# The first 2 MB store of a one-core residual matmul, issued as four transfers of 16, 16, 32 and 64 partitions

## The chip, the core and the metric

The kernel runs on one core of one Trainium2 chip. The metric is device time in microseconds (us). The kernel before takes 323.31 us, the median of three runs that lie between 323.17 and 324.18 us.

The core has a matmul engine (TensorE, in the profile PE), a vector engine (VectorE, DVE), a scalar engine (ACT), GpSimd (POOL) and a sync engine (SP). Here ACT does no arithmetic: it only issues loads. SP only issues the two small loads at the start and all stores. The transfers themselves run on 16 DMA engines that all transfers share. The on-chip memory that tiles live in has 128 partitions; PSUM is the accumulator memory that TensorE writes.

## The reference

`x` is 128 batches of 128 channels by 1024 time steps in float32, 64 MB in all. Each batch has a subject number between 0 and 7, and each subject has a 128x128 weight matrix.

```python
def _L0_cond_ref(x, subjects, weights):
    w = weights[subjects]
    out = jnp.einsum('bct,bcd->bdt', x, w)
    return out
x = x + _L0_cond_ref(x, itok_B_0_7, L0_cond_weights)
```

So each batch is multiplied by the matrix of its subject and added to itself. Every byte of `x` is read once and every byte of the result written once.

## The kernel before

**Tiling.** The work is done in 32 turns (`NT`). A turn is four batches, in two halves of two (`H = 2`, `G = 2`). One batch is a 128 x 1024 float32 tile of 512 KB, so a turn is 2 MB: 16 KB on each of the 128 partitions. `x_all` is one long tile that holds 12 turns (`SLOTS = 12`), and turn `i` lives in slot `i % 12`. The result is written over the input in the same slot, and the slot is stored from there.

**What the engines do in a turn.** VectorE copies the four weight matrices that this turn needs into `w` (line 159). TensorE multiplies each half with eight matmuls of 512 columns (line 168). VectorE adds the product from PSUM to the slot (line 180), once for each half, and so makes the slot's result.

**The loads.** ACT issues one transfer for each batch, 128 of 512 KB (lines 206 to 210, through `load`). They all go to ACT's DMA queue, which the profile calls q10. The first 48 need no wait, since 12 slots are free. From turn 12 on, ACT waits before the four loads of a turn until the slot's earlier store has landed. How far the slot's semaphore must have counted is what `emptied(i)` gives: every transfer adds 16, so one round of a slot is four loads and one store, 80. In slot 0 two of the first turn's loads count on another semaphore (`s_head`), which is why the formula has an exception there.

**The stores.** SP issues them (lines 219 to 223) to its own DMA queue, q1 in the profile. It waits until VectorE has added the turn and, up to the last turns, four turns more (`BEHIND = 4`): the store of turn 0 goes out when turn 4 has been added. Turns 0 to 19 are stored one by one, 2 MB each; the last 12 turns go in pairs of 4 MB. One store takes all 128 partitions; on the memory side each partition's 16 KB are four rows of 4 KB, one in each of the four batches.

**The order around the change.** All of it is written out by hand. SP's instructions are the two small loads, then wait and store, turn by turn. ACT's are the loads in order of turn with the waits on the slots. GpSimd waits for each turn's loads and tells TensorE (lines 212 to 217). The last store waits for nothing but its data and ends the program (line 243 on).

Of the kernel before, what the change touches and what calls it, by code (L numbers as in the profile page):

```python
# [30 lines left out]
G = 2  # L31
H = 2
# [3 lines left out]
SLOTS = 12  # L36
# [9 lines left out]
DMA = 16  # L46

IDLE = 3

ROWS = 4  # L50

# [4 lines left out]
def transfer(nc, engine, out, in_):  # L56

    later, nc._always_lower_symbolic_ap = nc._always_lower_symbolic_ap, False  # L60
    ins, outs = engine.lower_ap_dma(in_), engine.lower_ap_dma(out)
    nc._always_lower_symbolic_ap = later
    return engine.add_instruction(
        mybir.InstDMACopy(
            name=nc.get_next_instruction_name(),
            engine=engine.engine,
            ins=ins,
            outs=outs,
            mode="Copy",
            cce_op=ALU.bypass,  # L70
            queue=QUEUES[engine.engine],
        )
    )
# [3 lines left out]
def kernel(  # L77
# [7 lines left out]
    nc = tc.nc  # L85
    B, C, T = x.shape
    S, _, D = weights.shape
    NT = B // (G * H)

    def sbuf(name, *shape, dtype=F32):  # L90
        return ctx.enter_context(nc.sbuf_tensor(name, list(shape), dtype)).ap()
# [5 lines left out]
    x_all = sbuf("x_all", C, SLOTS * H * G * T)  # L97
# [23 lines left out]
    s_slot = [tc.alloc_semaphore(f"s_slot{k}") for k in range(SLOTS)]  # L121
    s_head = tc.alloc_semaphore("s_head")

    def emptied(i):
        turns = i // SLOTS
        return DMA * (H * G + 1) * turns - (DMA * G if i >= SLOTS and i % SLOTS == 0 else 0)

    def load(engine, i, q):
        transfer(
            nc,  # L130
            engine,
            xs[i % SLOTS][:, q, :],
            x[i * H * G + q].rearrange("(a r) t -> a (r t)", r=ROWS),
        ).then_inc(s_head if i * H * G + q < G else s_slot[i % SLOTS], DMA)

    def store(i, n):
        at = i % SLOTS * H * G * T
        return transfer(
            nc,
            nc.sync,  # L140
            out[i * H * G : (i + n) * H * G].rearrange("g d t -> d g t"),
            x_all[:, at : at + n * H * G * T].rearrange(
                "d (o t) -> d o t", o=1 if i >= NT - WHOLE else n
            ),
        )

    def subjects_of(i):
        _, subject = nc.values_load_multi_w_load_instructions(
            index[0:1, i] if isinstance(i, slice) else index[0:1, bass.ds(i * (H * G), H * G)],
            engines=[mybir.EngineType.DVE],  # L150
            min_val=0,
            max_val=S - 1,
            skip_runtime_bounds_check_because="the index is clamped on the chip above",
        )
        return subject

    def place(h, subject):
        for q in range(h * G, (h + 1) * G):
            copy = nc.vector.tensor_copy(ws[q], w_all[:, bass.ds(subject[q], 1), :])  # L159
        copy.then_inc(s_go, 1)  # L160

    def multiply(slot, h):
        nc.tensor.wait_ge(s_go, 1).then_inc(s_go, -1)
        nc.tensor.wait_ge(s_ready, 1).then_inc(s_ready, -1)  # L164
        for q in range(h * G, (h + 1) * G):
            for t in range(0, T, N):
                at = slot * (H * G * T) + (q * T + t)
                mm = nc.tensor.matmul(  # L168
                    ps[h][:, q % G, t : t + N],
                    ws[q][:, 0, :],  # L170
                    x_all[:, bass.ds(at, N)],
                    start=True,
                    stop=True,
                )
        mm.then_inc(s_product, 1)

    def add(slot, h):
        mine = x_all[:, bass.ds(slot * (H * G * T) + h * G * T, G * T)]
        nc.vector.wait_ge(s_product, 1).then_inc(s_product, -1)  # L179
        nc.vector.tensor_tensor(  # L180
            mine, ps[h].rearrange("d g t -> d (g t)"), mine, ALU.add
        ).then_inc(s_added, 1)

    with tc.tile_critical():  # L184

        nc.sync.dma_start(given, subjects.rearrange("(o b) -> o b", o=1)).then_inc(s_given, DMA)
        nc.sync.dma_start(w_all, weights.rearrange("s c d -> c s d")).then_inc(s_wall, DMA)

        nc.vector.memset(zeros, 0.0).then_inc(s_zeros, 1)  # L189
        nc.tensor.wait_ge(s_zeros, 1)  # L190
        for _ in range(IDLE):
            nc.tensor.matmul(  # L192
                ps[P_SLOTS - 1][:, G - 1, :N], zeros[:, :D], zeros, start=True, stop=True
            )

        nc.vector.memset(index[:, B:], 0).then_inc(s_index, 1)  # L199
        nc.vector.wait_ge(s_given, DMA)  # L200
        nc.vector.tensor_scalar(near, given, -S, S - 1, ALU.max, ALU.min).then_inc(s_index, 1)  # L201
        nc.vector.wait_ge(s_index, 2)
        nc.vector.tensor_scalar(wrap, near, 0, S, ALU.is_lt, ALU.mult).then_inc(s_index, 1)  # L203
        nc.vector.wait_ge(s_index, 3)
        nc.vector.tensor_tensor(index[:, :B], near, wrap, ALU.add).then_inc(s_index, 1)  # L205
        for i in range(NT):
            if i >= SLOTS:
                nc.scalar.wait_ge(s_slot[i % SLOTS], emptied(i))
            for q in range(H * G):
                load(nc.scalar, i, q)  # L210

        for i in range(NT):
            if i == 0:
                nc.gpsimd.wait_ge(s_head, DMA * G).then_inc(s_ready, 1)
                nc.gpsimd.wait_ge(s_slot[0], DMA * G).then_inc(s_ready, 1)
            else:
                nc.gpsimd.wait_ge(s_slot[i % SLOTS], emptied(i) + DMA * H * G).then_inc(s_ready, H)

        for i in [*range(NT - SLOTS), *range(NT - SLOTS, NT, PAIR)]:
            n = 1 if i < NT - SLOTS else PAIR  # L220
            nc.sync.wait_ge(s_added, (i + n + (BEHIND if i < NT - LAST else 0)) * H)
            if i + n < NT:
                store(i, n).then_inc(s_slot[i % SLOTS], DMA)


        nc.vector.wait_ge(s_index, 4)
        nc.vector.wait_ge(s_wall, DMA)
        subject = subjects_of(slice(0, H * G))
        for h in range(H):
            place(h, subject)  # L230
        with nc.vector.Fori(0, NT) as turn:  # L231
            subject = subjects_of(turn + 1)
            for h in range(H):
                add(turn % SLOTS, h)
                place(h, subject)
        with nc.tensor.Fori(0, NT) as turn:
            for h in range(H):
                multiply(turn % SLOTS, h)

    with tc.tile_critical() as waits:  # L240
        for i in range(NT - SLOTS, NT - PAIR, PAIR):
            nc.scalar.wait_ge(s_slot[i % SLOTS], emptied(i + SLOTS))
# [35 lines left out]
```

## Time and profile before

| what | value |
|---|---|
| median of three runs | 323.31 us |
| lowest and highest run | 323.17 and 324.18 us |
| span of the profiled execution, first to last instruction | 322.2 us |
| TensorE busy | 246.3 us (76% of the span) |
| VectorE busy | 165.7 us (51%) |
| bytes moved by DMA | 134.76 MB, 418 GB/s over the span |
| stores, 2 MB: from issue to landing, median | 17.0 us |
| loads, 512 KB: from issue to landing, median | 30.7 us |

For the profiled execution the profile gives the span alone; it is 1.1 us under the median of the runs, which also hold what lies around the first and the last instruction. A time in a row of the profile is counted from the span's start. "DMA share" is the mean busy share of the 16 DMA engines in a stretch (values a little over 1 come from transfers that are booked to the stretch in which they begin), and "GB/s" is what they moved together. SPq and ACTq are the instructions with which SP and ACT issue transfers.

### The profile page before, as it was taken

The numbers are of one execution on the slowest core, as the hardware profiler recorded it, in microseconds if no ns is written. First come the engines' busy times: TensorE is split into PE (matmuls) and PEld (weight loads), VectorE is DVE, ScalarE is ACT, GpSimd is POOL, SyncE is SP. The second block draws the span as 40 slices with busy tenths as digits, with TensorE's granted clock in tenths as the row PEclk, the third lists the DMA queues.
The fourth block names the chain that finished last, engine by engine and source line by source line (L and its number), as shares of the span: only waits on it lengthen the run. The fifth ranks groups of instructions, "written<-read, shape, count | busy, mean of one in ns | idle before, by whom it ended". The sixth has DMA issues, their size and how long they took to land. (4 is left out here: it accounts for less than half of the span.)

```text
span 322.2 us, 2368 instructions
## 1 busy us (share of the span) xinstructions
PE 246.3 (76%) x518; PEld 101.8 (32%) x518; DVE 165.7 (51%) x202; POOL 0.2 (0%) x4
## 2 busy tenths in 40 slices
PE   6999999999996974975987489885699994972000
PEld 2344444444442421331333134332244431430000
DVE  2276776777677345354355344762657666254000
POOL 0000000000000000000000000000000000000000
PEclk9799999999999797797899899997999998698555
DMA  7999999999999999999999999999999999999996
GB/s 271 425 429 429 425 423 401 429 425 423 425 423 427 430 431 429 423 425 423 427 421 429 429 433 427 423 425 423 427 423 429 429 431 427 427 435 433 419 427 264
DMA packets 11315, 134.76 MB, mean 418 GB/s; under 512 B 2481, under 2 KB 3506, under 8 KB 3506
## 3 DMA queue, kind: packets, MB, share of 16 engines
q10 hardware_dynamic: 6144, 67.12, 49.6%
q1 hardware_dynamic: 5170, 67.64, 49.5%
q14 instruction: 1, 0.01, 0.0%
HBM read 67.63 MB, written 67.11 MB: 418 GB/s over the span
## 5 line engine op out<-in xcount | busy, mean ns | idle before, releaser
L168 PE MATMUL ps<-x_all,w 128*128 x512 | 241.3, 629 | 44.1 <-PEq L164 38.4
L180 DVE TENSOR_TENSOR x_all<-ps,x_all 128x2048 f32 x64 | 146.7, 2292 | 122.7 <-DVEq L179 122.7
L168 PEld LDWEIGHTS ps<-x_all,w 128*128 128x128 f32 x512 | 100.0, 201 | 185.7 <-issue 185.2
L159 DVE COPY w<-w_all 128x128 f32 x132 | 23.2, 219 | 4.7 <-DMA w_all<-in_L_cond_weights_dram 4.7
L192 PE MATMUL ps<-zeros 128*128 128x512 f32 x6 | 4.9, 988 | 1.7 <-DVE zeros L189 1.7
L192 PEld LDWEIGHTS ps<-zeros 128*128 128x128 f32 x6 | 1.8, 328 | 3.7 <-issue 2.1
L189 DVE MEMSET zeros<- 128x512 f32 x1 | 0.5, 485 | 1.0 <-SPq L184 1.0
L201 DVE TENSOR_SCALAR near<-given 1x128 int32<-1x128 int32 x1 | 0.2, 214 | 0.6 <-DMA given<-in_itok_B_dram 0.6
L205 DVE CUSTOM_DVE_ANT_0 index<-near,wrap 1x256 uint16<-1x256 uint16 x1 | 0.3, 280 | 0.0
L203 DVE TENSOR_SCALAR wrap<-near 1x128 int32<-1x128 int32 x1 | 0.2, 215 | 0.0
L265 POOL MEMSET const-bfloat16-1.0<- 128x1 bf16 x1 | 0.1, 102 | 0.0
L265 POOL MEMSET const-uint8-127<- 128x1 uint8 x1 | 0.1, 102 | 0.0
L265 POOL MEMSET const-float32-0.0<- 128x1 f32 x1 | 0.1, 99 | 0.2 <-issue 0.2
L265 POOL MEMSET const-float32-1.0<- 128x1 f32 x1 | 0.1, 99 | 0.0
L265 DVE BASE_LOAD x1 | 0.0, 21 | 0.1
L199 DVE MEMSET index<- 1x4 int32 x1 | 0.1, 62 | 0.0
## 6 DMA issues: line engine op xcount, KB each, us to landing
x_all<-in_x_dram ACTq DMA_DIRECT2D x128, 512.0 KB, 30.7
out_dram<-x_all SPq DMA_DIRECT2D x20, 2048.0 KB, 17.0
out_dram<-x_all SPq DMA_DIRECT2D x6, 4096.0 KB, 30.5
w_all<-in_L_cond_weights_dram SPq DMA_DIRECT2D x1, 512.0 KB, 5.5
given<-in_itok_B_dram SPq DMA_DIRECT2D x1, 0.5 KB
```

Source lines behind the costliest of these rows:

```text
L159: copy = nc.vector.tensor_copy(ws[q], w_all[:, bass.ds(subject[q], 1), :])
L168: mm = nc.tensor.matmul(ps[h][:, q % G, t : t + N], ws[q][:, 0, :], x_all[:, bass.ds(at, N)], start=True, stop=True,)
L180: nc.vector.tensor_tensor(mine, ps[h].rearrange("d g t -> d (g t)"), mine, ALU.add).then_inc(s_added, 1)
L189: nc.vector.memset(zeros, 0.0).then_inc(s_zeros, 1)
L192: nc.tensor.matmul(ps[P_SLOTS - 1][:, G - 1, :N], zeros[:, :D], zeros, start=True, stop=True)
L199: nc.vector.memset(index[:, B:], 0).then_inc(s_index, 1)
L201: nc.vector.tensor_scalar(near, given, -S, S - 1, ALU.max, ALU.min).then_inc(s_index, 1)
L203: nc.vector.tensor_scalar(wrap, near, 0, S, ALU.is_lt, ALU.mult).then_inc(s_index, 1)
L205: nc.vector.tensor_tensor(index[:, :B], near, wrap, ALU.add).then_inc(s_index, 1)
L265: nc = _bacc.Bacc("TRN2", target_bir_lowering=False, num_devices=1)
```

## The change

The store of turn 0, and only that, is issued as four transfers in place of one. They take partitions 0 to 15, 16 to 31, 32 to 63 and 64 to 127 of slot 0, each with all four batches: 256 KB, 256 KB, 512 KB and 1 MB. All four add to the slot's semaphore, so that turn 12's load waits for 96 instead of 48. No other instruction differs, on any engine.

```diff
 IDLE = 3
+
+PARTS = (16, 16, 32, 64)
...
     def emptied(i):
         turns = i // SLOTS
-        return DMA * (H * G + 1) * turns - (DMA * G if i >= SLOTS and i % SLOTS == 0 else 0)
+        first = DMA * (len(PARTS) - 1 - G) if i >= SLOTS and i % SLOTS == 0 else 0
+        return DMA * (H * G + 1) * turns + first
...
+    def store_rows(i, d, n):
+        at = i % SLOTS * H * G * T
+        return transfer(
+            nc,
+            nc.sync,
+            out[i * H * G : (i + 1) * H * G, d : d + n].rearrange("g d t -> d g t"),
+            x_all[d : d + n, at : at + H * G * T].rearrange("d (o t) -> d o t", o=1),
+        )
...
             nc.sync.wait_ge(s_added, (i + n + (BEHIND if i < NT - LAST else 0)) * H)
-            if i + n < NT:
+            if i == 0:
+                for k, rows in enumerate(PARTS):
+                    store_rows(i, sum(PARTS[:k]), rows).then_inc(s_slot[0], DMA)
+            elif i + n < NT:
                 store(i, n).then_inc(s_slot[i % SLOTS], DMA)
```

## The prediction

> **What bounds the kernel now.** I read the page's slices and queues first, because 134.76 MB in 322.2 us is suspiciously close to a plain copying rate.
>
> ```profile
> span 322.2 us, 2368 instructions
> ...
> DMA  7999999999999999999999999999999999999996
> GB/s 271 425 429 429 425 423 401 429 425 423 425 423 427 430 431 429 423 425 423 427 421 429 429 433 427 423 425 423 427 423 429 429 431 427 427 435 433 419 427 264
> DMA packets 11315, 134.76 MB, mean 418 GB/s; under 512 B 2481, under 2 KB 3506, under 8 KB 3506
> ## 3 DMA queue, kind: packets, MB, share of 16 engines
> q10 hardware_dynamic: 6144, 67.12, 49.6%
> q1 hardware_dynamic: 5170, 67.64, 49.5%
> ```
>
> The 16 DMA engines are busy in every slice but the first and the last, at 420 to 435 GB/s, whichever queue feeds them. One slice in the middle stands out: the seventh, 401 GB/s, which is 48.3 to 56.4 us. So I asked for the same numbers by stages.
>
> ```profile
> core 0: us, PE busy (x) PEld busy (x) DVE busy (x) POOL busy (x), PEclk, DMA share, GB/s
> 2.00:6.00 4.00, 4.00 (x5) 1.50 (x5) 0.71 (x3) 0.00 (x0) 1.00 1.00 322
> 6.00:46.00 40.00, 37.83 (x83) 15.58 (x82) 23.69 (x31) 0.00 (x0) 0.96 1.01 426
> 46.00:51.00 5.00, 5.00 (x12) 2.15 (x12) 3.78 (x4) 0.00 (x0) 1.00 1.00 423
> 51.00:56.00 5.00, 5.00 (x13) 2.01 (x11) 3.90 (x6) 0.00 (x0) 1.00 1.00 387
> 56.00:66.00 10.00, 10.00 (x25) 4.28 (x24) 7.24 (x7) 0.00 (x0) 1.00 0.99 423
> 66.00:116.00 50.00, 45.01 (x99) 18.54 (x97) 33.11 (x40) 0.00 (x0) 0.97 1.01 428
> 116.00:284.00 168.00, 131.97 (x272) 54.45 (x272) 85.66 (x103) 0.00 (x0) 0.92 1.01 426
> 284.00:320.00 36.00, 7.13 (x16) 2.96 (x16) 7.12 (x9) 0.00 (x0) 0.67 0.99 420
> 320.00:322.20 2.20, 0.00 (x0) 0.00 (x0) 0.00 (x0) 0.00 (x0) 0.50 0.00 0
> ```
>
> From 6 to 320 us the rate is that of saturated engines: about 426 GB/s with loads alone (6 to 46), with both kinds (66 to 284) and nearly so with stores alone (284 to 320). TensorE and VectorE have idle time in every long stage. The consequence for the sum: any microsecond in which all 16 engines move nothing comes back at the end as a microsecond, and a transfer that is merely earlier or later, while the other queue has work, costs nothing. The one place of waste in the middle is 51 to 56 us: 387 instead of 426 GB/s over 5 us, that is 5 x (1 - 387/426) = 0.46 us. What happens there is the first store:
>
> ```profile
> engine op xcount: duration ns min/median/max, first and last start us, forms
> L63 SPq DMA_DIRECT2D out_dram<-x_all x1: 652/652/652, 48.4 to 48.4; - x1
> ...
> DMA to landing us min/median/max: 14.1/14.1/14.1
> ```
>
> ```profile
> 45.45 17.53 ACTq L63 DMA_DIRECT2D x_all<-in_x_dram  x2
> ```
>
> ```profile
> 52.00:53.00 1.00, 1.00 (x4) 0.25 (x3) 0.34 (x3) 0.00 (x0) 1.00 0.49 180
> 245.00:250.00 5.00, 5.00 (x13) 1.99 (x11) 3.86 (x6) 0.00 (x0) 1.00 1.00 426
> ```
>
> SP issues it at 48.37 us in 0.65 us, its data land 14.1 us later, and ACT, which had issued its 48 free loads by 46.5 us, issues the next one when it lands (the row of ACT joins two loads, 45.45 and 62.48 us, because nothing lies between them). The microsecond from 52 to 53 has 180 GB/s: there the store's first data meet the loads. When the store queue starts again after a pause, at 246 us, the rate stays at 426. So the hole belongs to the first store, and I do not know its cause.
>
> **The change part by part.**
>
> *Issue on SP: nothing.* Three transfers more, at the 0.54 us that a later store's issue takes (last row below) to the 0.65 us above, are 1.6 to 2.0 us of SP's time. SP is free until 55.47, when turn 5 has been added; it spends its life in waits:
>
> ```profile
> engine line waited for: us in total, times, longest us
> SPq L63 <- DVE x_all L180: 264.9, 24, 46.6
> ```
>
> ```profile
> L63 SPq DMA_DIRECT2D out_dram<-x_all x1: 538/538/538, 55.5 to 55.5; - x1
> ```
>
> The fourth part is issued at about 50.2 us, 5 us ahead of the next store. Without that cover the 2 us would delay store 1 alone, whose data wait in a queue behind store 0 anyway.
>
> *When the data move: nothing by itself.* Until 52.4 us the load queue alone moves data, 4.0 us after the issue; the first bytes of the store queue are in the next stretch:
>
> ```profile
> DMA packets 142, 1.56 MB, mean 389 GB/s; under 512 B 47, under 2 KB 47, under 8 KB 47
> q10 hardware_dynamic: 142, 1.56, 101.5%
> ```
>
> ```profile
> DMA packets 18, 0.18 MB, mean 300 GB/s; under 512 B 7, under 2 KB 7, under 8 KB 7
> q1 hardware_dynamic: 8, 0.13, 50.9%
> q10 hardware_dynamic: 10, 0.05, 30.0%
> ```
>
> (48.4 to 52.4, then 52.4 to 53.0 us.) If a 16-partition part needs less than 4 us to its first byte, that is no gain: loads fill the time.
>
> *The wait of turn 12's load: nothing.* It now needs all four parts. After 62.5 us both queues have work (56 to 62 us: the store queue 1.43 MB, the load queue 1.18 MB), and a load issued at 62.48 lands only 22.0 us later because others stand ahead of it. A start that is a few us later finds neither queue empty; only a delay that outlasts that stock, most of 22 us, would idle engines for the rest of it.
>
> ```profile
> q1 hardware_dynamic: 103, 1.43, 55.6%
> q10 hardware_dynamic: 110, 1.18, 46.2%
> ```
>
> ```profile
> x_all<-in_x_dram ACTq DMA_DIRECT2D x1, 512.0 KB, 22.0
> ```
>
> *The reads of four narrow bands: the term that decides.* A store of 128 partitions gives each of the 16 engines 8 partitions, so the engines together draw on the whole memory. One engine's pace is 426/16 = 26.6 GB/s, or 16 KB (one partition of slot 0) in 0.615 us, call it p. In the change a part of 16 partitions gives each engine one partition: all 16 engines read from a band that a single store gave to two of them. Part 3 gives each engine two partitions, part 4 four. How fast 16 engines read a band of 16 partitions, the trace of before does not show. Bounds from its rows:
>
> - Lower end of the cost: a band is read as fast as the whole, 0 us; and if small parts also remove the hole, -0.46 us.
> - Upper end: eight partitions give no more than the one pace that the trace shows for them. Then 16 partitions give two paces. Each engine alternates between the two queues (the two shares above are near equal), so of its time beside the store a turn goes to a load. Parts 1 and 2: eight engines for each pace, one packet each: 8p = 4.92 us in place of 2p for a load and a store packet, so 6p = 3.69 us lost in each. Part 3: four engines for each pace, two packets each: 8p in place of 4p, 2.46 us. Part 4: two engines for each pace, with every second turn a load: nothing, when they take turns. Together 3.69 + 3.69 + 2.46 = 9.8 us.
>
> Between 0 and 9.8 I take four paces for a band of 16 partitions, near the geometric middle of two and sixteen (5.7), on the low side: the row of 180 GB/s is the nearest evidence, and it says that packets of the one queue do hold up those of the other. At four paces: parts 1 and 2 have four engines for each pace, 4p in place of 2p, so 2p = 1.23 us lost in each; part 3 has two engines for each pace, covered by alternation, 0; part 4 likewise, 0. Sum +2.46 us; if alternation doesn't stagger the engines, part 3 and 4 add to it.
>
> The hole: I keep it (0), because nothing in the rows ties it to the size of the transfer.
>
> *Sum.* 322.2 + 2.5 = 324.7 us of span; with the 1.1 us by which the median of the runs exceeds the span, 323.3 + 2.5 = 325.8 us.
>
> [...] No run of before shows a narrow transfer.
>
> **The rivals.**
>
> *A: a narrow band costs nothing* (not slower than before). The engines fetch ahead while the other queue's data move, so a slow read of one packet is hidden by a load. For it: in 46 to 51 and 56 to 66 us the rate is the same, 423, with one queue and with two. Then the change is 0, or the hole goes too: 323.3 - 0.46 = 322.85 us. It decides if 16 engines on 16 partitions run at over half of 426 GB/s. Against it: the dip to 180 shows that queues disturb each other.
>
> *B: the engines stall in step, in all four parts.* If a slow read holds the engine's load as well, alternation staggers nothing, and if part 4 reaches only half of the paces, it pays too. With four paces for 16 partitions, eight each for 32 and for 64: parts 1 and 2 take 4p for p, part 3 takes 4p for 2p, part 4 takes 8p for 4p: 3p + 3p + 2p + 4p = 12p = 7.4 us, 330.7 us. Against it: staggering is likely, since the engines' phases differ. [...] With half of these losses hidden behind loads it is 327.0.
>
> *C: each part pays the first store's hole.* Each part's data come to an empty queue and disturb the loads as in 51 to 56 us: three more holes, 3 x 0.46 = 1.4 us, 324.7 us. Against it: 426 GB/s at the restart at 246 us.
>
> *The change doesn't do what it says:* the hole has no tie to the store's size, so removing it may fail; that is the upper half of A, 323.3 us.
>
> **How the numbers follow.** Chances: narrow bands with staggered engines 0.40 (its own range 324.3 to 327.5), A 0.30 (322.5 to 324.3), B 0.18 (327 to 331), C 0.12 (324.3 to 325.2). The time predicted is that of the likeliest, 325.8. From 322.7 to 328.2 leaves out the lower edge of A (about 0.05) and more than half of B (0.13). 0.3% is 0.97 us, about what a measurement of this kernel can tell from no change. Faster than 322.34 needs more than the hole gives: 0.02. Within 322.34 to 324.28 lies A: 0.29. Slower: 0.69, the rest.
>
> **What would show it.** In the stage table of the changed kernel 51 to 56 us falls below 387 GB/s, to about 426 x (1 - 2.9/5) = 180, or the loss spreads to 58 us; after that 423 to 428 as before; all later stages are shifted by the same 2.5 us, and the end with them. The first and second part land 2 us or more after their first bytes. If narrow bands cost nothing, the stage keeps 387 or rises to 423. If the loss is in every part, rates stay low to 60 us and beyond. The prediction fails if a band of 16 partitions is read at the full rate, or if the reads of one queue stall the other for a whole part.

## The result and the profile after

The changed kernel takes 328.01 us (median of six runs, 327.06 to 329.98) against 323.25 us before (median of six runs, three of them those of the table above). The ratio is 1.0149, with a 95% interval of 1.0131 to 1.0167: slower by 1.5%, 4.8 us. The profiled execution took 327.94 us, its span is 326.2 us, 4.0 us longer than that of before. The profiled execution of before was a long one. In every run on record that lists both, the time is 1.7 to 1.9 us above the span, so a span of 322.2 us stands for a time of about 324.0 us (an estimate from that gap), not for the median of 323.3; 61 further executions of the same kernel, run beside the experiments below, have spans of 321.1 to 322.1 us, with a median of 321.5. Against 321.5 the span has grown by 4.7 us. The runs also scatter more: 2.9 us between the lowest and the highest, where those of before lie within 1.1 us.

The slices of the changed kernel, from its page:

```profile
span 326.2 us, 2371 instructions
...
DMA  7999999999999999999999999999999999999993
GB/s 281 422 422 442 420 420 370 408 424 422 420 424 432 416 421 424 424 420 424 422 410 436 424 424 426 430 426 424 430 426 428 424 430 426 424 440 436 422 430 153
```

The seventh slice has fallen from 401 to 370 GB/s and the last from 264 to 153. The same stages as in the prediction:

```profile
core 0: us, PE busy (x) PEld busy (x) DVE busy (x) POOL busy (x), PEclk, DMA share, GB/s
46.00:51.00 5.00, 5.00 (x12) 2.00 (x11) 3.03 (x7) 0.00 (x0) 1.00 1.03 423
51.00:56.00 5.00, 5.00 (x13) 2.27 (x12) 3.87 (x4) 0.00 (x0) 1.00 1.03 347
56.00:66.00 10.00, 10.00 (x23) 4.01 (x22) 7.26 (x10) 0.00 (x0) 1.00 1.00 408
66.00:116.00 50.00, 42.51 (x93) 17.77 (x92) 29.34 (x35) 0.00 (x0) 0.93 1.01 423
116.00:284.00 168.00, 132.96 (x269) 54.87 (x268) 84.95 (x103) 0.00 (x0) 0.90 1.01 425
284.00:320.00 36.00, 10.15 (x24) 3.95 (x22) 10.13 (x12) 0.00 (x0) 0.72 1.00 428
320.00:326.20 6.20, 0.00 (x0) 0.00 (x0) 0.00 (x0) 0.00 (x0) 0.50 0.19 79
```

Against the rows of before, each taken as length x (rate before - rate after)/426: 51 to 56 us loses 5 x 40/426 = 0.47 us more than before, 56 to 66 loses 0.35, 66 to 116 loses 0.59 and 116 to 284 loses 0.39. That is 1.8 us, and only 0.8 of it lies near the split store. The last term is one unit of a rounded rate; the bytes themselves give nearly the same: the 22.38 MB that before has moved by 56 us, after has moved by about 56.4, and the 83.80 MB of 200 us by 201.9; from there on the distance stays 1.9 us. The other 2.2 us of the 4.0 lie at the very end. The last microseconds in steps of two, first before, then after:

```profile
316.00:318.00 2.00, 0.00 (x0) 0.00 (x0) 0.00 (x0) 0.00 (x0) 0.50 1.04 442
318.00:320.00 2.00, 0.00 (x0) 0.00 (x0) 0.00 (x0) 0.00 (x0) 0.50 0.46 197
320.00:322.00 2.00, 0.00 (x0) 0.00 (x0) 0.00 (x0) 0.00 (x0) 0.50 0.00 0
```

```profile
318.00:320.00 2.00, 0.00 (x0) 0.00 (x0) 0.00 (x0) 0.00 (x0) 0.50 0.88 377
320.00:322.00 2.00, 0.00 (x0) 0.00 (x0) 0.00 (x0) 0.00 (x0) 0.50 0.39 164
322.00:324.00 2.00, 0.00 (x0) 0.00 (x0) 0.00 (x0) 0.00 (x0) 0.50 0.19 82
324.00:326.00 2.00, 0.00 (x0) 0.00 (x0) 0.00 (x0) 0.00 (x0) 0.50 0.00 0
```

Before, the 16 DMA engines stop nearly together: full rate until 318 us, then nothing after 320. After, the rate comes down by a staircase, 377, 164, 82 GB/s, at a mean busy share of 0.88, 0.39 and 0.19: fewer and fewer engines work on. The trace's landing events say the same. Each store has 16 of them, as many as there are engines. Those of the last store lie within 1.76 us of each other before, and within 5.07 us after; the mean of the 16 moved by 1.9 us, the last of them by 3.9. The time of the kernel is that of the last. The engines that end late are probably those that were held up, but the trace names no engine, so that is not shown.

Around the split store, the first part and the microseconds from 51 to 55; then the same microseconds before, of which the prediction shows the one from 52 to 53:

```profile
L65 SPq DMA_DIRECT2D out_dram<-x_all x1: 702/702/702, 46.1 to 46.1; - x1
...
DMA to landing us min/median/max: 6.3/6.3/6.3
```

```profile
51.00:52.00 1.00, 1.00 (x4) 0.46 (x3) 1.00 (x1) 0.00 (x0) 1.00 1.93 459
52.00:53.00 1.00, 1.00 (x4) 0.49 (x3) 1.00 (x1) 0.00 (x0) 1.00 0.50 213
53.00:54.00 1.00, 1.00 (x3) 0.30 (x2) 0.41 (x3) 0.00 (x0) 1.00 0.83 328
54.00:55.00 1.00, 1.00 (x4) 0.52 (x4) 0.46 (x1) 0.00 (x0) 1.00 0.84 295
```

```profile
51.00:52.00 1.00, 1.00 (x4) 0.49 (x3) 1.00 (x2) 0.00 (x0) 1.00 1.49 475
53.00:54.00 1.00, 1.00 (x3) 0.50 (x4) 0.85 (x1) 0.00 (x0) 1.00 1.17 475
54.00:55.00 1.00, 1.00 (x3) 0.38 (x2) 1.00 (x1) 0.00 (x0) 1.00 0.76 328
```

A DMA share of 1.93 at an ordinary 459 GB/s means transfers that began in that microsecond and lasted far beyond it: engines that are busy and don't get on. Over the four microseconds the mean is 324 GB/s, against 365 before. The rows of before also put the 180 GB/s of 52 to 53 us, on which the prediction leaned, in its place: the microsecond ahead of it has a share of 1.49, so a part of the dip is only the way in which transfers are booked; the two together moved 328 GB/s, not 180.

### The profile page after: what moved, and what is told of

Read it like the earlier page. It is cut to its first block, busy times and chain, and to the rows that moved or that the text cites. A ratio compares the mean times of both kernels' runs of the same rounds, so it can differ in the third digit from the quotient of the medians.

```text
span 326.2 us, 2371 instructions
## 1 busy us (share of the span) xinstructions
PE 248.6 (76%) x518; PEld 102.7 (31%) x518; DVE 165.7 (51%) x202; POOL 0.2 (0%) x4
```

## The experiments

Theory 1 is that of the prediction: reads of a narrow band hold engines up; to it came, from the staircase, that some engines fall behind and stay behind. Theory 2 is rival C, a price for each transfer that comes to an empty queue. Theory 3 puts the loss down to the first store as such.

**Four transfers, but all 128 partitions.** The store is cut by batch instead of by partition.

```diff
-PARTS = (16, 16, 32, 64)
+PARTS = (1, 1, 1, 1)
...
-            out[i * H * G : (i + 1) * H * G, d : d + n].rearrange("g d t -> d g t"),
-            x_all[d : d + n, at : at + H * G * T].rearrange("d (o t) -> d o t", o=1),
+            out[i * H * G + g : i * H * G + g + n].rearrange("g d t -> d g t"),
+            x_all[:, at + g * T : at + (g + n) * T].rearrange("d (o t) -> d o t", o=1),
...
```

> The store of turn 0 is again four transfers, but each takes all 128 partitions and one of the four batches (512 KB each). Theory 1, narrow bands (16 engines that read few partitions hold each other up, some engines fall several us behind, and the last store ends with the slowest of them): no narrow band is left, so 323.3 us, at most 0.5 us off, and the last store's data end within 2 us of each other. Theory 2, each transfer that comes to an empty store queue costs a hole of 0.46 us: 323.3 + 3 x 0.46 = 324.7 us. If smaller first transfers remove the hole: 322.8 us.

Measured: 323.17 us against 323.41, ratio 0.9993 (0.9984 to 1.0002). Its stages around the store, and ACT's first load that had to wait:

```profile
46.00:51.00 5.00, 5.00 (x13) 2.10 (x12) 3.12 (x6) 0.00 (x0) 1.00 0.99 405
51.00:56.00 5.00, 5.00 (x12) 2.15 (x12) 3.78 (x4) 0.00 (x0) 1.00 1.00 419
56.00:66.00 10.00, 10.00 (x24) 4.17 (x23) 7.26 (x10) 0.00 (x0) 1.00 1.01 424
```

```profile
69.41 2.83 ACTq L65 DMA_DIRECT2D x_all<-in_x_dram  x4
```

Four transfers cost nothing, so theory 2 falls. The hole of before (387 GB/s from 51 to 56 us) is smaller, not gone: that stage has 419 here, but the one ahead of it has 405 where before had 423 (the first part was issued 2 us earlier here). Over the ten microseconds the mean is 412 instead of 405 GB/s, and the time shows no gain beyond its interval. The shares of the last store land within 1.33 us of each other, as theory 1 expected (within 2). And turn 12's load was released at 69.4 us, 7 us later than before, without any loss: the wait of that load is not what costs.

**Two halves, and eight parts of 16.** In the changed kernel, one constant each:

```diff
-PARTS = (16, 16, 32, 64)
+PARTS = (64, 64)
```

> The store of turn 0 is two transfers of 64 partitions. Theory 1 with the pace going by the number of partitions down to 64: half the engines' paces are there for 16 engines, loads fill every second turn, so between 323.3 (staggered) and, with 4 + 4 packets at double time in step, 323.3 + 4.9 = 328.2 us; I expect about 325. Theory 2: one more hole, 323.8 us.

```diff
-PARTS = (16, 16, 32, 64)
+PARTS = (16,) * 8
```

> The store of turn 0 is eight transfers of 16 partitions. Theory 1: parts 1 and 2 are those of the change, six more of the same kind follow: 8 x 1.23 = 9.8 us over before by the staggered sum, 333 us, and more if the engines run in step. Theory 2: seven more holes, 323.3 + 3.2 = 326.5 us, below the changed kernel's 328.0. If the loss of the change came from its 64-partition part alone: about 323.3 us.

Measured: the halves 325.26 us, ratio 1.0047 (1.0032 to 1.0061); the eight parts 326.26 us, ratio 1.0081 (1.0066 to 1.0095). Each of these cuts across the partitions costs time, as theory 1 says, and the halves as much as it expected; but the eight parts cost 2.6 us (0.0081 x 323.3), not 9.8, and less than the change. That expectation was missed by far, and the 326.5 us that theory 2 gave is what came; theory 2 has fallen with the four transfers by batch all the same. The sum over parts isn't additive. One thing differs visibly in the eighths: SP's issues take up to 2.2 us where those of before take 0.54 to 0.65, so the parts are issued over 10 us, from 48.1 to 58.0 (the ninth in the row, at 59.6, is the store of turn 1):

```profile
L65 SPq DMA_DIRECT2D out_dram<-x_all x9: 577/1591/2169, 48.1 to 59.6; - x9
```

That this spacing is why they cost less was not tried.

**The disputed cost by itself.** Before the last store the engines run empty; then single transfers follow, each after the landing of the one before. They write results of turns 28 and 29 a second time.

```diff
+PROBES = ((0, 128, 1), (0, 64, 2), (64, 64, 2), (0, 32, 4), (0, 16, 8), (16, 16, 8), (0, 128, 8))
...
+        k = 0
+        for i in range(NT - SLOTS, NT - PAIR, PAIR):
+            nc.sync.wait_ge(s_slot[i % SLOTS], emptied(i + SLOTS))
+        for d, rows, nb in PROBES:
+            at = (NT - 4) % SLOTS * H * G * T
+            i = (NT - 4) * H * G
+            for _ in range(2):
+                k += 1
+                transfer(
+                    nc,
+                    nc.sync,
+                    out[i : i + nb, d : d + rows].rearrange("g d t -> d g t"),
+                    x_all[d : d + rows, at : at + nb * T].rearrange("d (o t) -> d o t", o=1),
+                ).then_inc(s_probe, DMA)
+                nc.sync.wait_ge(s_probe, DMA * k)
```

> Before the last store the DMA engines are let run empty, and then seven transfers, each made twice and each waiting for the one before, write a stored pair of turns again (extra work, so the time of the whole kernel is not compared): 128 partitions x 4 KB, 64 x 8 KB from partition 0, 64 x 8 KB from 64, 32 x 16 KB, 16 x 32 KB from 0, 16 x 32 KB from 16 (512 KB each) and 128 x 32 KB (4 MB). From issue to landing: theory 1 with four paces for 16 partitions and eight for 32 and 64: 1.2 us of data time for 128 partitions, 2.5 for 64 and 32, 4.9 for 16, all on top of the same fixed time. With two paces for 16: 9.8 us. Theory 2 (no narrow bands): all 512 KB transfers within 0.5 us of each other.

The transfers of 512 KB by their start, with the time to landing below each: 128 partitions (310.5), 64 (316.4), 32 (333.5) and 16 (342.1).

```profile
L65 SPq DMA_DIRECT2D out_dram<-x_all x1: 482/482/482, 310.5 to 310.5; - x1
DMA to landing us min/median/max: 2.9/2.9/2.9
...
L65 SPq DMA_DIRECT2D out_dram<-x_all x1: 565/565/565, 316.4 to 316.4; - x1
DMA to landing us min/median/max: 4.3/4.3/4.3
...
L65 SPq DMA_DIRECT2D out_dram<-x_all x1: 596/596/596, 333.5 to 333.5; - x1
DMA to landing us min/median/max: 4.3/4.3/4.3
...
L65 SPq DMA_DIRECT2D out_dram<-x_all x1: 551/551/551, 342.1 to 342.1; - x1
DMA to landing us min/median/max: 6.8/6.8/6.8
```

If all 128 partitions are read at 426 GB/s, 512 KB are 1.2 us, so the fixed part is 1.7 us (the 4 MB of all 128 landed after 11.6 us, and by the same rate that leaves 1.8), and the data take 1.2, 2.6, 2.6 and 5.1 us: 1 to 2 to 2 to 4. With sixteen paces for all 128, by this estimate, sixteen neighbouring partitions are read at four, 32 and 64 both at eight. The transfers from partition 64 and from 16 land after 4.2 and 6.8 us too.

**The place of the partitions, by itself.** The same, with partitions taken in steps.

```diff
-        for d, rows, nb in PROBES:
+        for d, rows, step, nb in PROBES:
...
-                    out[i : i + nb, d : d + rows].rearrange("g d t -> d g t"),
-                    x_all[d : d + rows, at : at + nb * T].rearrange("d (o t) -> d o t", o=1),
+                    out[i : i + nb, d : d + rows * step : step].rearrange("g d t -> d g t"),
+                    x_all[d : d + rows * step : step, at : at + nb * T].rearrange("d (o t) -> d o t", o=1),
```

> As the transfers measured alone, 512 KB each and each twice, the time of the whole kernel not compared: 16 partitions with a step of 1, 4 and 8; 32 with a step of 1 and 4; 64 with a step of 1 and 2. If the number of partitions sets the pace: all of 16 land after 6.8 us, all of 32 and 64 after 4.3. If their place does: 16 in steps of 4 or 8 like 32 side by side, 4.3 us; 32 in steps of 4 and 64 in steps of 2 between 2.9 (like all 128) and 4.3 us.

Sixteen partitions in steps of 1, 4 and 8 land after 6.8, 4.1 and 4.2 us, 64 in steps of 1 and 2 after 4.3 and 3.0. The rows for 32 partitions, in steps of 1 (341.1) and 4 (349.7):

```profile
L65 SPq DMA_DIRECT2D out_dram<-x_all x1: 567/567/567, 341.1 to 341.1; - x1
DMA to landing us min/median/max: 4.3/4.3/4.3
...
L65 SPq DMA_DIRECT2D out_dram<-x_all x1: 564/564/564, 349.7 to 349.7; - x1
DMA to landing us min/median/max: 3.0/3.0/3.0
```

Thirty-two partitions land after 3.0 us if they are every fourth one, where all 128 took 2.9 us and 32 neighbours 4.3. Not the number decides but the place. By the estimate above (1.7 us fixed, 1.2 us of data at sixteen paces) 16 in steps of 4 or 8 are read at about eight paces, where 16 neighbours have four, and every fourth or every second of 128 at about fifteen. What in the memory makes the place count is not shown: the runs show the times alone.

**The place in the kernel.** Four transfers of 32 partitions for the first store, once as neighbours and once every fourth:

```diff
-PARTS = (16, 16, 32, 64)
+PARTS = (32, 32, 32, 32)
```

> The store of turn 0 is four transfers of 32 neighbouring partitions each. Measured alone, 32 neighbours take twice as long to read as all 128. Theory 1: a loss like that of the two halves, which also run at half the pace, 324.5 to 327 us. It is the partner of the next kernel.

```diff
-            out[i * H * G : (i + 1) * H * G, d : d + n].rearrange("g d t -> d g t"),
-            x_all[d : d + n, at : at + H * G * T].rearrange("d (o t) -> d o t", o=1),
+            out[i * H * G : (i + 1) * H * G, d::n].rearrange("g d t -> d g t"),
+            x_all[d::n, at : at + H * G * T].rearrange("d (o t) -> d o t", o=1),
...
-                for k, rows in enumerate(PARTS):
-                    store_rows(i, sum(PARTS[:k]), rows).then_inc(s_slot[0], DMA)
+                for k in range(len(PARTS)):
+                    store_rows(i, k, len(PARTS)).then_inc(s_slot[0], DMA)
```

> The store of turn 0 is four transfers of 32 partitions each, every fourth partition (0, 4, 8 and so on, then 1, 5, 9 and so on). The same number of transfers, partitions and bytes as with 32 neighbours; only the place differs, and measured alone such a transfer is as fast as one of 128. Theory 1 in the form that the place of the partitions sets the pace: 323.2 us, within 0.5. If the number of partitions in a transfer matters: 324.5 to 327 us like its partner.

Measured: neighbours 323.97 us, ratio 1.0020 (1.0010 to 1.0031); every fourth 323.11 us, ratio 0.9999 (0.9989 to 1.0008). The price of the neighbours is small, 0.65 us, below the 324.5 to 327 us that I expected, but it is there, and with the same number of transfers, partitions and bytes it goes away when the place is changed. Parts of 16 were not run in both places in the kernel; for them the place is shown by the transfers measured alone (6.8 us for 16 neighbours, 4.1 in steps of 4). How the engines end does not tell the two runs apart: neighbours, and below them every fourth, both move nothing after 320 us, and the shares of the last store land 1.89 and 1.06 us apart.

```profile
318.00:320.00 2.00, 0.00 (x0) 0.00 (x0) 0.00 (x0) 0.00 (x0) 0.50 0.43 180
320.00:322.00 2.00, 0.00 (x0) 0.00 (x0) 0.00 (x0) 0.00 (x0) 0.50 0.00 0
```

```profile
318.00:320.00 2.00, 0.00 (x0) 0.00 (x0) 0.00 (x0) 0.00 (x0) 0.50 0.31 131
320.00:322.00 2.00, 0.00 (x0) 0.00 (x0) 0.00 (x0) 0.00 (x0) 0.50 0.00 0
```

**Which parts.** Two changes of the constant: the first two parts as they are and the rest in one, and the first two joined.

```diff
-PARTS = (16, 16, 32, 64)
+PARTS = (16, 16, 96)
```

> Parts 1 and 2 as in the change, then one transfer of the other 96 partitions, which reach both halves of the memory. Theory 1: if the first two narrow parts bring most of the loss, about 326 to 328 us; by the staggered sum of the prediction 2 x 1.23 = 2.5 us, 325.8. If the parts of 32 and 64 partitions, whose packets follow one another on an engine, bring most of it, 324 us or less. Theory 2, a hole for each transfer: 324.2 us, ruled out by the four transfers by batch, which cost nothing.

```diff
-PARTS = (16, 16, 32, 64)
+PARTS = (32, 32, 64)
```

> The store of turn 0 is three transfers of 32, 32 and 64 partitions: the change with its two parts of 16 joined to one of 32. Four parts of 32 cost 0.7 us and two of 64 cost 2.0. If the parts of 16 bring most of the change's 4.7 us: 323.5 to 324.8 us here. If the last part of 64, or the step from small to large parts, brings it: 326 to 328 us.

Measured: (16, 16, 96) 327.39 us, ratio 1.0143 (1.0096 to 1.0191), as slow as the change within the interval; (32, 32, 64) 324.61 us, ratio 1.0046 (1.0034 to 1.0058). Joining the two parts of 16 takes 3.3 us of the 4.8 away. Three parts of 32, 32 and 64 still cost 1.5.

**Another store.** The split moved from turn 0 to turn 5, whose store comes when both queues run.

```diff
 PARTS = (16, 16, 32, 64)
+AT = 5
...
-            if i == 0:
+            if i == AT:
...
```

> The split in 16, 16, 32 and 64 partitions is moved from the store of turn 0 to that of turn 5, which comes when both queues run. Theory 1: the same narrow reads, so a loss of the same kind, 325 to 328 us. Theory 3, the loss belongs to the first store, where the stores' queue begins from nothing: 323.3 us, within 0.5.

Measured: 327.55 us, ratio 1.0147 (1.0121 to 1.0174). The same loss at another store: theory 3 falls.

**No loads beside.** The split moved to the 4 MB store of turns 28 and 29.

```diff
+AT = 28
...
-            out[i * H * G : (i + 1) * H * G, d : d + n].rearrange("g d t -> d g t"),
-            x_all[d : d + n, at : at + H * G * T].rearrange("d (o t) -> d o t", o=1),
+            out[i * H * G : (i + PAIR) * H * G, d : d + n].rearrange("g d t -> d g t"),
+            x_all[d : d + n, at : at + PAIR * H * G * T].rearrange("d (o t) -> d o t", o=1),
...
-            if i == 0:
+            if i == AT:
...
```

> The store of turn 0 is one transfer again, and the store of turns 28 and 29 (4 MB), which runs when no loads are left, is split into 16, 16, 32 and 64 partitions. Measured alone the parts would take 5.2 + 5.2 + 5.2 + 10.4 = 26 us of data time where the single store takes 9.9: 16 us more if the parts run one after the other; less where engines that are through with one part begin the next. If loads between the narrow reads hid most of their price in the change, the loss here is well over the change's 4.7 us (with twice the bytes in each part, over 9.4): 333 to 339 us. If loads hid nothing, about twice the change's loss, 332 us, or less.

Measured: 336.54 us, ratio 1.0399 (1.0370 to 1.0427), 12.9 us slower by the ratio. Its last stages, then two of before:

```profile
300.00:310.00 10.00, 0.00 (x0) 0.00 (x0) 0.00 (x0) 0.00 (x0) 0.50 0.93 203
310.00:320.00 10.00, 0.00 (x0) 0.00 (x0) 0.00 (x0) 0.00 (x0) 0.50 1.02 275
320.00:330.00 10.00, 0.00 (x0) 0.00 (x0) 0.00 (x0) 0.00 (x0) 0.50 0.69 272
330.00:338.00 8.00, 0.00 (x0) 0.00 (x0) 0.00 (x0) 0.00 (x0) 0.50 0.13 57
```

```profile
300.00:310.00 10.00, 0.00 (x0) 0.00 (x0) 0.00 (x0) 0.00 (x0) 0.50 1.03 439
310.00:320.00 10.00, 0.00 (x0) 0.00 (x0) 0.00 (x0) 0.00 (x0) 0.50 0.89 380
```

Busy engines (0.93 to 1.02) at 203 and 275 GB/s where before moved 439 and, its end included, 380, and again a tail: the shares of the last store land 16.0 us apart. The time lies within the 333 to 339 us that I gave for loads hiding most of the price. The size says less than that. If the loss goes by the bytes, which no run tests, one turn's share is half, 6.5 us, against 4.8 with loads beside: about a quarter hidden, and not most of it.

**Two transfers of two batches**, 128 partitions each, as a candidate that might beat both kernels. The edit is made in the kernel of the four transfers by batch:

```diff
-PARTS = (1, 1, 1, 1)
+PARTS = (2, 2)
```

> The store of turn 0 is two transfers of two batches each, all 128 partitions (1 MB each). Theory 1: no narrow band, no loss: 322.8 to 323.4 us. If the hole at the first store goes away with a smaller first transfer, as in the trace of the four transfers by batch, at most 0.5 us less than before.

Measured: 323.18 us against 323.20, ratio 0.9994 (0.9985 to 1.0003). No gain that can be told from none.

## Why the prediction was right, and where its size was off

The time came out the way that was forecast, slower, and for the reason given, narrow reads. But 328.01 us lies only 0.2 us inside the upper end of the stated 322.7 to 328.2, above the 324.3 to 327.5 that the prediction gave to its own theory, and within the 327 to 331 of rival B. That the range covers it is in part luck.

- **The bound.** Right: the DMA engines are the bound (busy shares of 0.99 to 1.01 in the stages of before from 6 to 320 us), and time in which they move less comes back at the end (the 83.80 MB of 200 us came 1.9 us later, and the distance stayed). What the statement missed is that "the end" is that of the slowest engine, not of the mean (the last share of the last store moved by 3.9 us, the mean of the 16 by 1.9).
- **Issue on SP, the moment the data move, the wait of turn 12's load: nothing.** The runs agree. In the change the fourth issue took 1.5 us, more than the 0.65 allowed, and still ended 3.6 us ahead of the next store, at 53.2. Four transfers by batch have as many issues and a release 7 us later and cost nothing.
- **The reads of narrow bands: the term that decides.** Right in kind: place alone, with all else equal, makes the difference between 1.0020 and 0.9999. Right in pace for 16 partitions: I took four paces between two and sixteen, and measured alone it is four (5.1 us for 512 KB, against 1.2). No row of before gave the four; it was a choice between two bounds. Nor does the trace name an engine: that each engine takes 8 partitions of a store and one of a part of 16 was my estimate, from its 128 or 16 packets of 16 KB and the 16 landings of each. The sign named for it came, too: the first part was issued at 46.1 us and landed 6.3 us later, at 52.4, over 2 us after the store queue's first data at 49.5 to 50.2.
- **The size was off by two: 2.5 us predicted, 4.8 measured.** The term mis-sized is "parts 1 and 2 ... 2p = 1.23 us lost in each; part 3 ... 0; part 4 likewise, 0". Parts 1 and 2 in the place of one part of 32 cost 3.3 us instead of 2.46. Parts of 32 and 64 are not free: (32, 32, 64) costs 1.5 us, two halves 1.5. I gave 64 partitions sixteen engines in turns on eight paces and let alternation cover it exactly. Alternation was read from two near-equal shares of the queues (55.6 and 46.2%) and is not shown engine by engine, and no row of before gave the eight paces for 64; measured alone, 64 neighbours land after 4.3 us, as 32 do. Against the run without loads, loads hide about a quarter, if the loss goes by the bytes. Nor is 1.23 us a fixed price of a part of 16: eight of them cost 2.6 us together, about 0.3 each.
- **What the sum left out: the engines fall out of step.** I averaged the loss over the engines. Of the 4.0 us of span only 1.8 is a lower rate anywhere; 2.2 us is the staircase at the end. A transfer has landed only when the last of its 16 shares has: the semaphore counts 16 for it, and the span ended 4.0 us later where the last share of the last store came 3.9 us later. The staircase does not come with the split as such: the last store's shares land 1.33 us apart after four transfers by batch, 1.06 after four of every fourth partition and 2.43 after two of two batches (1.76 before). Nor does it come with every narrow band: 32 neighbours (1.89) and (32, 32, 64) (1.83) have none. It is seen where parts of 16 or two halves were cut: 5.07 in the change, 5.24 in the eighths, 4.53 at turn 5, 3.83 with the halves, 3.27 with (16, 16, 96). These are one trace each; that of two batches is the slowest of its eleven runs, that of (32, 32, 64) the fastest of its six.
- **"51 to 56 us falls ... to about 180"** was wrong: it fell to 347, and later stages did not stay as before but lost 0.35, 0.59 and 0.39 us more. The prediction's sign for a loss in every part, low rates to 60 us and beyond, is what came (408 GB/s from 56 to 66 us, against 423).
- **The hole, kept in the sum**: as far as the times show, that was right. With four transfers by batch it is smaller (412 instead of 405 GB/s from 46 to 56 us) and the time doesn't show the difference. The hole was read in an execution of before that was some 0.7 us longer than usual; that the others have it is not shown.
- **Rivals.** A (nothing) is ruled out by the result (1.0149) and by the pair that differs in place alone (1.0020 and 0.9999), C (a hole for each transfer) by the four transfers by batch (0.9993). B had the paces right, eight for 64 as for 32 (4.3 us each, measured alone; for B they were a supposition), and was right that parts of 32 and 64 pay (1.5 us for 32, 32 and 64), but not in its full price: 7.4 us in step, where 4.8 was lost with loads and 6.5 for the same bytes without. What happened lies between the prediction's own theory and B.

Three things stay open. Eight parts of 16 cost less (2.6 us) than two of 16 with one of 96 (4.6); the wider spacing of the eight, or the part of 96, may be why. The lower rate between 66 and 284 us, long after the split store has landed, is seen in the trace but its cause was not tested; from 116 to 284 us the four runs with parts of 16 for a 2 MB store move 424 to 425 GB/s, the others 426 to 427. And why some cuts leave the engines out of step and others not was not tested.

## What to carry to other kernels

Cut a transfer along the free axis, not across partitions: four pieces of 128 partitions cost nothing here, four of 16 to 64 neighbours cost 1.5% of the whole kernel, four of 32 neighbours 0.2%. If it must be fewer partitions, spread them (every fourth of 128 landed after 3.0 us alone, all 128 after 2.9, and four such parts in the kernel gave 0.9999), and measure such a transfer alone first: landing times of 2.9, 4.3 and 6.8 us told in one run which parts are slow, though not how much the kernel would lose by them. Look also at where the profiled execution lies among the runs before you read a small hole in it. In a kernel bound by DMA look at how the engines end, too: a staircase in the last microseconds is time that an average over the engines does not show, 2.2 us of 4.0 here.

## What was not expected of the hardware

One 2 MB store, split at about 46 us, still shows some 275 us later in a last store whose 16 shares land 5.07 us apart, instead of 1.76. The distance does not stand at every store between. The shares of the stores of turns 1 to 11 land 3.5 to 4.1 us apart (1.5 to 1.9 before), those of turns 14 to 20 only 0.6 to 1.1 (0.8 to 0.9 before), and those of the last four 5.1 (1.8 before). In turns 18 to 23 it is the loads that land apart: the last 16 landings of a turn's loads lie 3.7 to 8.6 us apart (1.7 to 4.2 before). So the engines seem to stay out of step while the distance moves from one queue to the other; the trace names no engine, so this is a reading and not shown. And the scatter of the runs grows with it, from 1.1 us to 2.9.
